# A second block by maxima in one of four graphs, and six generators under way, in the first stage of a four-layer graph network

## The chip, the cores and the metric

The kernel runs on one core of a Trainium2 chip. The metric is the device time in microseconds, the median of several runs. A core has five engines that matter here: TensorE (PE in the profile; its weight loads are shown apart as PEld), VectorE (DVE), ScalarE (ACT), GpSimd (POOL) and SyncE (SP), which only issues transfers. Each engine takes its own instructions strictly in order and waits on semaphores for the others.

## The reference, cut to what matters

Four layers over 128 graphs of 128 nodes with 128 features; each normalizes its input, cuts it at zero and adds a graph layer's result. The change touches only the first half of layer 0, which scores every pair of nodes:

```python
h = jnp.maximum(_layernorm(x, axis=-1), 0.0)
D = jnp.abs(x[:, :, None, :] - x[:, None, :, :])      # x is h here
h = jnp.einsum('bijc,oc->bijo', D, W1) + b1            # 64 outputs for each pair
m = jnp.mean(h, axis=(0, 1, 2))
v = jnp.mean((h - m) ** 2, axis=(0, 1, 2))
h = (h - m) / jnp.sqrt(v + EPS) * g1 + be1
```

The mean and variance go over all pairs of all graphs, so nothing after them can begin until every pair of every graph has been made once. What follows (a leaky relu, a product with W2, a masked softmax, and the three further layers) is the same code before and after.

## The kernel before, in words

The distance is symmetric, so only 127/256 of the ordered pairs of a graph are made: node i with the 63 or 64 nodes after it, cyclically. For that each graph's features, transposed so that features lie on partitions, are kept 192 columns wide in a tile `he`, whose last 64 columns repeat the first 64. A graph's pairs are four blocks `q` of 32 rows each; blocks 0 and 1 are 64 pairs wide (2048 columns), blocks 2 and 3 are 63 (2016).

The first stage has two kinds of generator. `nodes(g)` prepares a group of four graphs: load, normalize (DVE, POOL), transpose (PE into the PSUM tile `pt`), relu on ACT into `he` and once more into `pt`, store to DRAM for later. POOL makes the wrapped columns (`wrapped`, L510 to L512), beside PE's product of the group's features with W1 (`pu`, L496), which ACT and DVE then split into three bf16 parts `us` (L499 to L505). `pairs(b)` handles one graph: its four blocks run as `block(b, q, made)`, and their statistics are put together at the end (L523). The pairs go to DRAM (tile `v`, L526), except for those of the last eight graphs, which stay.

A block is made in one of two ways:

- By differences (blocks 1, 2, 3): DVE (L545) or POOL (L548) subtracts into a tile `d`, ACT takes the absolute value in place (L551), and PE multiplies by W1 (L565, four fp32 matmuls).
- By maxima (block 0): |a - b| = 2 max(a, b) - a - b. DVE makes the maximum (L545, the same instruction form as the subtraction), ACT has nothing to do, and PE multiplies it by 2 W1 and adds the correction -W1 a - W1 b in twelve further bf16 matmuls: the three parts `us` of W1 h, against a constant tile `both` that holds -1 at the two nodes of each pair.

Either way PE leaves 128x1008 or 128x1024 in the PSUM tile `ph`, ACT copies it to `v` (L575), and DVE takes batch statistics of it in two instructions (L580). In every graph DVE makes block 0; in three of four graphs it makes block 2 as well, in the fourth POOL does; POOL makes blocks 1 and 3.

The order of each engine's instructions is fixed while the program is built, by the planner `in_order` (L51): each generator yields an engine, an estimated work time, and the buffers that the step takes and frees; at most `A_UNDER_WAY` generators are open at once; the step that can begin first by these estimates goes next, and the older generator at equal times. Buffers: five `d`, three `ph`, eight `v`, two each of `he`, `pt`, `us`. At run time the order stays as written, with semaphore waits where data or buffers need them.

Of the kernel before, what the change touches and what calls it, by code (L numbers as in the profile page):

```python
# [9 lines left out]
F32 = mybir.dt.float32  # L10
I32 = mybir.dt.int32
I16 = mybir.dt.int16
BF16 = mybir.dt.bfloat16
AF = mybir.ActivationFunctionType
ALU = mybir.AluOpType
# [3 lines left out]
P = 128  # L19
EPS = 1e-5  # L20
NEG = -9000000000000000.0
W = 192
QR = 32
NQ = P // QR
GS = 8
GB = 4
# [6 lines left out]
C_T, C_W, C_V, C_O, C_M = 28, 11, 3, 6, 7  # L33
C_KEPT = {"ps": 1, "t": 6, "w": 3, "v": 1}
A_D = 5
A_UNDER_WAY = 4
A_KEPT = {}
KEEP = 8
B_V, B_R = 8, 3
# [7 lines left out]
PE, ACT, DVE, POOL, DMA = "PE", "ACT", "DVE", "POOL", "DMA"  # L47
# [105 lines left out]
def bcast(ap, pos, n):  # L153

    dims = [list(d) for d in ap.ap]
    return bass.AP(tensor=ap.tensor, offset=ap.offset, ap=dims[:pos] + [[0, n]] + dims[pos:])
# [3 lines left out]
def kernel(ctx: ExitStack, tc: tile.TileContext, x, adj, w, out):  # L160
    nc = tc.nc
# [7 lines left out]
    def cst(name, shape, dtype=F32):  # L169
        return const.tile(shape, dtype, tag=name, name=name)  # L170
# [41 lines left out]
    w1T = cst("w1T", [P, 64])  # L212
# [24 lines left out]
    with tc.tile_pool(name="wload", bufs=2) as wl, tc.tile_pool(  # L237
        name="wps", bufs=2, space=PSUM
# [191 lines left out]
    with tc.tile_pool(name="h_pool", bufs=1) as h_pool, tc.tile_pool(name="pairs", bufs=B_V) as b_v:  # L430
# [10 lines left out]
        with tc.tile_pool(name="a2", bufs=2) as a2, tc.tile_pool(  # L441
            name="a_d", bufs=A_D
        ) as a_d, tc.tile_pool(name="a_ph", bufs=3, space=PSUM) as a_ph, tc.tile_pool(
            name="a_ps", bufs=2, space=PSUM
# [14 lines left out]
            w1T2 = a2.tile([P, 64], F32, tag="w1T2", name="w1T2", bufs=1)  # L459
            nc.vector.tensor_scalar(w1T2, w1T, 2.0, None, ALU.mult)  # L460

            def nodes(g):

                b0 = g * GB
                yield DMA, 0.6, "xg", ""
                xg = a2.tile([P, GB, P], F32, tag="xg", name="xg")
                nc.sync.dma_start(xg, x_t[:, b0 : b0 + GB, :])
                yield DVE, 1.3, "", ""
                s6 = a2.tile([P, GB, 6], F32, tag="ln_s6", name="ln_s6")
                mv = a2.tile([P, GB, 2], F32, tag="ln_mv", name="ln_mv")  # L470
                for i in range(GB):
                    nc.vector.bn_stats(s6[:, i, :], xg[:, i, :])
                    nc.vector.bn_aggr(mv[:, i, :], s6[:, i, :])

                yield POOL, 3.3, "xn", "xg"
                rs = a2.tile([P, GB], F32, tag="ln_rs", name="ln_rs")
                nc.gpsimd.tensor_tensor(rs, mv[:, :, 1], eps, ALU.add)
                nc.gpsimd.tensor_tensor(rs, rs, nhalf, ALU.pow)
                xn = a2.tile([P, GB, P], F32, tag="ln_xn", name="ln_xn")
                nc.gpsimd.tensor_tensor(xn, xg, bcast(mv[:, :, 0], 2, P), ALU.subtract)  # L480
                nc.gpsimd.tensor_tensor(xn, xn, bcast(rs, 2, P), ALU.mult)
                yield PE, 0.45, "pt", "xn"
                pt = a_ps.tile([P, GB, P], F32, tag="pt", name="pt")
                for i in range(GB):
                    nc.tensor.transpose(pt[:, i, :], xn[:, i, :], ident)
                yield ACT, 1.0, "he", ""
                he = a2.tile([P, GB, W], F32, tag="he", name="he")
                nc.scalar.activation(he[:, :, 0:P], pt, AF.Relu)
                nc.sync.dma_start(h_d[g], he[:, :, 0:P])
                nc.scalar.activation(pt, pt, AF.Relu)  # L490
                yield "fork", wrapped(g, he)

                yield PE, 0.9, "ph us", ""
                pu = a_ph.tile([P, GB, 64], F32, tag="ph", name="pu")
                for i in range(GB):
                    nc.tensor.matmul(pu[:, i, :], he[:, i, 0:P], w1T, start=True, stop=True)  # L496
                us = a2.tile([P, 3, GB, 64], BF16, tag="us", name="us")
                yield ACT, 0.31, "", ""
                nc.scalar.copy(us[:, 0], pu)  # L499
                yield DVE, 0.36, "", ""  # L500
                nc.vector.tensor_tensor(pu, pu, us[:, 0], ALU.subtract)
                yield ACT, 0.31, "", ""
                nc.scalar.copy(us[:, 1], pu)
                yield DVE, 0.34, "", "ph"
                nc.vector.tensor_tensor(us[:, 2], pu, us[:, 1], ALU.subtract)  # L505
                yield "join",
                ready[g] = he, pt, us
                yield "done", ("nodes", g)

            def wrapped(g, he):  # L510
                yield POOL, 0.42, "", ""
                nc.gpsimd.tensor_copy(he[:, :, P:W], he[:, :, 0 : W - P])  # L512

            def pairs(b):
                made = {"six": a2.tile([P, 2 * NQ, 6], F32, tag="six", name="six", bufs=4)}
                for q in range(NQ):
                    yield "fork", block(b, q, made)
                yield "join",
                left[b // GB] -= 1
                if not left[b // GB]:  # L520
                    yield "free", "he pt us"
                yield DVE, 0.37, "", ""
                nc.vector.bn_aggr(st[:, b, :], made["six"].rearrange("p a b -> p (a b)"))  # L523
                if b < NB - KEEP:
                    yield DMA, 5.0, "", "v"
                    nc.sync.dma_start(pairs_d[b], made["v"])  # L526
                else:
                    here[b] = made["v"]

            def block(b, q, made):  # L530

                w_, i0, n = width[q], QR * q, 8 * width[q]
                by_dve = q == 0 or (q == 2 and b % 4 != 3)
                yield "after", ("nodes", b // GB)
                yield (DVE, 2.17, "d", "") if by_dve else (POOL, 3.58, "d", "")
                hb, hp, us = (t[..., b % GB, :] for t in ready[b // GB])
                d = a_d.tile([P, QR * 64], F32, tag="d", name="d")  # L540
                dv = d[:, 0 : 4 * n].rearrange("p (i j) -> p i j", j=w_)
                later = shifted(hb[:, i0 + 1 : i0 + 1 + w_], QR)
                if by_dve:
                    own = bcast(hp[:, i0 : i0 + QR], 2, w_)
                    nc.vector.tensor_tensor(dv, later, own, ALU.subtract if q else ALU.max)  # L545
                else:
                    own = bcast(hb[:, i0 : i0 + QR], 2, w_)
                    nc.gpsimd.tensor_tensor(dv, later, own, ALU.subtract)  # L548
                if q:
                    yield ACT, 1.82, "", ""  # L550
                    nc.scalar.activation(d[:, 0 : 4 * n], d[:, 0 : 4 * n], AF.Abs)  # L551
                yield PE, 1.73 if q else 3.15, "ph", "d"
                ph = a_ph.tile([P, 2, 512], F32, tag="ph", name="ph")
                every4 = "p (r x j) -> p x r j"
                by_part = d[:, 0 : 4 * n].rearrange(every4, x=4, j=w_)
                both_by_part = both.rearrange(every4, x=4, j=64)
                for part in range(1 if q else 4):
                    for t in range(2):
                        for a in range(2):
                            k = 2 * t + a  # L560
                            if part == 0:
                                wt, x_ = w1T if q else w1T2, by_part[:, k]
                            else:
                                wt, x_ = us[:, part - 1, :], both_by_part[:, k]
                            nc.tensor.matmul(  # L565
                                ph[64 * a : 64 * a + 64, t, 0:n], wt, x_,
                                start=part == 0, stop=q > 0 or part == 3,
                            )
                if q:
                    yield "after", ("v", b)  # L570
                yield ACT, 0.93, "" if q else "v", "ph"
                if q == 0:
                    made["v"] = b_v.tile([P, NPAIR], F32, tag="v", name="v")
                v = made["v"][:, first[q] : first[q] + 2 * n]
                nc.scalar.copy(v.rearrange("p (t e) -> p t e", t=2), ph[:, :, 0:n])  # L575
                if q == 0:
                    yield "done", ("v", b)
                yield DVE, 1.19, "", ""
                for t in range(2):
                    nc.vector.bn_stats(made["six"][:, 2 * q + t, :], v[:, t * n : t * n + n])  # L580

            ready, left = {}, [GB] * (NB // GB)
# [6 lines left out]
            with tc.manual_schedule(engines=ORDERED):  # L589
                in_order(makers, A_UNDER_WAY, {"d": A_D, "ph": 3, "v": B_V} | two, A_KEPT)  # L590

# [13 lines left out]
            own = a2.tile([P, 1], F32, tag="own", name="own")  # L605
# [4 lines left out]
                start=True, stop=True,  # L610
# [12 lines left out]
        with tc.tile_pool(name="b2", bufs=2) as b2p, tc.tile_pool(name="b_s", bufs=2, space=PSUM) as b_s, tc.tile_pool(  # L623
            name="b_ps", bufs=6, space=PSUM
# [17 lines left out]
                start=True, stop=True,  # L642
# [745 lines left out]
```

## Time and profile before

| what | value |
|---|---|
| median of three runs | 3178.52 us (3177.65 to 3181.38) |
| profiled execution, its own time | 3173.2 us |
| its span, first to last instruction | 3171.4 us |
| first stage: first block's max starts, last graph's statistics end | 40.1 us, 1261.5 us |
| busy in the stage from 40 to 1240 us: PE, DVE, ACT, POOL | 1118.41, 1177.10, 1183.27, 1117.67 of 1200 us |
| instructions in the whole kernel: subtract or max on DVE, on POOL, absolute values | 224, 288, 384 |

Busy time is the union of an engine's instructions: where two overlap, the stretch counts once. The mean of a group is the time of one instruction from start to end, and with pipelining it is longer than the pitch from start to start. "Idle before" is the time in which the engine stood still ahead of an instruction, put down to what came last. In groups, `out<-in` names the tiles, followed by partitions x elements, then the count, busy time and mean.

### The profile page before, as it was taken

Reading aid. Unit: us, or ns where it says so; the run is one execution under the profiler, and the core shown is the slowest. Engines: PE = TensorE matmul, PEld = TensorE weight load, DVE = VectorE, ACT = ScalarE, POOL = GpSimd, SP = SyncE. Lnnn points to the kernel's source line nnn. Section 1 sums busy time; section 2 is a strip of 40 time slices with the busy share of each in tenths; the row PEclk is TensorE's granted clock in tenths of the full one; section 3 lists DMA queues with packets and bytes.
Section 4 is the critical chain, followed back from the end, with each engine's and each line's share of the span. In section 5 each row is a group of like instructions: output and inputs, shape, how many; then the busy total and the mean of one; then the engine's idle time right before and its main releaser. Section 6 shows DMA issues by size and latency. Waiting matters only on the chain.

```text
span 3171.4 us, 46611 instructions
## 1 busy us (share of the span) xinstructions
PE 2832.2 (89%) x17129; PEld 1559.5 (49%) x17129; DVE 2657.7 (84%) x4730; ACT 2673.4 (84%) x3082; POOL 1495.2 (47%) x953
## 2 busy tenths in 40 slices
PE   6999999999999998888888898789999999999996
PEld 2333333333333333233333333367777777877774
DVE  6999999999999998777787787667788878888864
ACT  5999999999999999987787887557877878887774
POOL 5999999999999996111111111122213222212211
PEclk8999999999999999999999998889999999999997
DMA  3555555555555550999999999420111111111000
GB/s 115 226 244 242 240 227 225 243 230 231 240 228 224 237 239 36 373 404 395 401 394 400 404 406 398 151 70 21 51 31 47 42 39 36 54 31 41 11 11 12
DMA packets 150718, 606.46 MB, mean 191 GB/s; under 512 B 15633, under 2 KB 99026, under 8 KB 119762
## 3 DMA queue, kind: packets, MB, share of 16 engines
q1 hardware_dynamic: 140242, 569.86, 45.6%
q0 software_dynamic: 10240, 33.53, 2.9%
q8 instruction: 139, 2.28, 0.3%
q14 instruction: 97, 0.79, 0.1%
HBM read 322.74 MB, written 280.61 MB: 190 GB/s over the span
## 4 chain that ended last, share of the span: by engine, by line
PE 27%; DVE 13%; issue 7%; ACT 5%; POOL 2%; DMA 1%; POOLq 0%; DVEq 0%; ACTq 0%
PE pa L1091 5%; PE sc L698 4%; PE po L1006 2%; DVE p L962 2%; PE z L958 1%; PE ps L1110 1%; PE pl L787 1%; PE pp L1103 1%; PE ph L1233 1%; DMA s<-us 1%; PE pl L789 1%; DVE s L928 1%; DVE v L425 1%; DVE xh L1015 1%; DVE f1d L1194 1%
## 5 line engine op out<-in xcount | busy, mean ns | idle before, releaser
L548 POOL TENSOR_TENSOR d<-he 128x2016 f32<-128x2016 f32 (+1 forms) x288 | 1022.0, 3578 | 77.6 <-ACT v L575 61.7
L565 PE MATMUL ph<-d,w1T 128*64 128x512 f32 (+1 forms) x4096 | 939.8, 596 | 83.1 <-ACT d L551 40.6
L551 ACT ACTIVATE d<-d 128x2016 f32<-128x2016 f32 (+1 forms) x384 | 741.1, 1932 | 0.1
L580 DVE BATCH_NORM_STATS2 six<-v 128x6 f32<-128x504 f32 (+1 forms) x1024 | 631.5, 670 | 8.7 <-ACT v L575 5.1
L565 PEld LDWEIGHTS ph<-d,w1T 128*64 128x64 f32 x4096 | 306.4, 136 | 613.7 <-issue 385.3
L575 ACT COPY v<-ph 128x1024 f32<-128x1024 f32 (+1 forms) x512 | 517.1, 1035 | 14.6 <-PE ph L565 14.6
L545 DVE TENSOR_TENSOR d<-he,pt 128x2048 f32<-128x2048 f32 (+1 forms) x224 | 506.1, 2259 | 13.0 <-PE ph L565 13.0
L935 POOL TENSOR_TENSOR rs<-ve,nhalf 128x4 f32<-128x4 f32 x96 | 120.0, 1250 | 772.2 <-DVE ve L932 558.1
L425 DVE SCALAR_TENSOR_TENSOR v<-v 128x1528 f32<-128x1528 f32 x256 | 433.9, 1742 | 32.8 <-ACT v L653 32.2
L653 ACT ACTIVATE v<-v,h_bi,h_sc 128x1528 f32<-128x1528 f32 x256 | 413.2, 1662 | 6.8 <-DVE h_bi L417 6.8
L698 PE MATMUL sc<-v,w_slide 128*32 128x512 f32 (+1 forms) x1536 | 321.4, 599 | 17.2 <-DVE v L425 16.9
L1091 PE MATMUL pa<-vals,p 128*128 128x99 f32 (+2 forms) x2048 | 254.9, 280 | 14.3 <-DVE p L962 11.1
L1091 PEld LDWEIGHTS pa<-vals,p 128*128 128x128 f32 x2048 | 249.2, 197 | 32.7 <-DVE p L962 15.1
L698 PE MATMUL sc<-v,w_line 128*32 128x504 f32 x512 | 260.3, 590 | 0.0
L698 PE MATMUL sc<-r,w_relu 128*32 128x504 f32 x512 | 258.2, 586 | 0.0
L962 DVE SCALAR_TENSOR_TENSOR p<-p,q 128x1024 f32<-128x1024 f32 (+1 forms) x192 | 206.2, 1081 | 49.5 <-ACT q L1078 24.9
L565 PE MATMUL ph<-both,us 128*64 128x512 bf16 x1536 | 190.5, 381 | 0.0
L1077 ACT ACTIVATE p<-z 128x1024 f32<-128x1024 f32 x128 | 133.2, 1040 | 35.0 <-PE z L958 34.5
L565 PEld LDWEIGHTS <-us 128*64 128x64 bf16 x1536 | 100.9, 111 | 117.7 <-issue 74.6
L660 ACT ACTIVATE r<-v,h_bi,h_sc 128x1008 f32<-128x1008 f32 x128 | 157.4, 1229 | 0.0
L799 ACT ACTIVATE e<-e 128x512 f32<-128x512 f32 x32 | 20.2, 630 | 149.3 <-DVE e L797 149.3
L698 PEld LDWEIGHTS sc<-v,w_slide 128*32 128x32 f32 x1536 | 65.1, 109 | 158.9 <-DVE v L425 82.5
(253 smaller groups left out, 4501.9 us busy)
## 6 DMA issues: line engine op xcount, KB each, us to landing
v<-v SPq DMA_DIRECT2D x240, 2032.0 KB, 9.1
xg<-in_x SPq DMA_DIRECT2D x64, 256.0 KB, 3.1
ht<-h SPq DMA_DIRECT2D x64, 256.0 KB, 6.4
u<-s POOLq DMA_DIRECT2D x16, 768.0 KB, 11.6
h<-he SPq DMA_DIRECT2D x32, 256.0 KB, 3.5
adj<-in_adj SPq DMA_DIRECT2D x32, 256.0 KB, 3.0
adj<-in_adj POOLq DMA_DIRECT2D x32, 256.0 KB, 8.6
y<-yt POOLq DMA_DIRECT2D x32, 256.0 KB, 7.1
```

The costliest lines, as they stand in the source:

```text
L425: engine.scalar_tensor_tensor(out, v, slope, v, ALU.mult, ALU.max)
L545: nc.vector.tensor_tensor(dv, later, own, ALU.subtract if q else ALU.max)
L548: nc.gpsimd.tensor_tensor(dv, later, own, ALU.subtract)
L551: nc.scalar.activation(d[:, 0 : 4 * n], d[:, 0 : 4 * n], AF.Abs)
L565: nc.tensor.matmul(ph[64 * a : 64 * a + 64, t, 0:n], wt, x_, start=part == 0, stop=q > 0 or part == 3,)
L575: nc.scalar.copy(v.rearrange("p (t e) -> p t e", t=2), ph[:, :, 0:n])
L580: nc.vector.bn_stats(made["six"][:, 2 * q + t, :], v[:, t * n : t * n + n])
L653: nc.scalar.activation(part, part, AF.Identity, bias=h_bi, scale=h_sc)
L660: nc.scalar.activation(made["r"][:, 0:n], part, AF.Relu, bias=h_bi, scale=h_sc)
L698: nc.tensor.matmul(sc[rows, 0:n], wz[:, 31 - k : 63 - k], z, start=begins and q < NQ, stop=ends and q != NQ - 1, tile_position=(0, rows.st ...
L962: nc.vector.scalar_tensor_tensor(p, p, FLOOR, q, ALU.max, ALU.max)
L1091: nc.tensor.matmul(pa_all[:, h * (DH + 1) : h * (DH + 1) + n], p[:, h, :], vals_all[:, e : e + n], start=True, stop=True,)
```

## The change

In each group of four graphs, block 1 of the first graph is now also made by maxima. Its correction needs W1 times the graph's nodes turned by 32, so that the same constant tile `both` serves; `pu` and `us` get a fifth part for it, from columns 32 to 159 of `he`, and the wrapped columns must therefore be there first: POOL's copy moves from a branch of its own into the sequence ahead of the `pu` matmuls. The subtractions are shared out anew: DVE makes block 2 in the second and fourth graph of a group, POOL in the first and third. At most six generators are open instead of four, and the statistics tiles `six` have six buffers.

```diff
-A_UNDER_WAY = 4
+A_UNDER_WAY = 6
...
-                yield "fork", wrapped(g, he)
-
-                yield PE, 0.9, "ph us", ""
-                pu = a_ph.tile([P, GB, 64], F32, tag="ph", name="pu")
+                yield POOL, 0.42, "", ""
+                nc.gpsimd.tensor_copy(he[:, :, P:W], he[:, :, 0 : W - P])
+
+
+                yield PE, 1.1, "ph us", ""
+                pu = a_ph.tile([P, GB + 1, 64], F32, tag="ph", name="pu")
                 for i in range(GB):
                     nc.tensor.matmul(pu[:, i, :], he[:, i, 0:P], w1T, start=True, stop=True)
-                us = a2.tile([P, 3, GB, 64], BF16, tag="us", name="us")
+                nc.tensor.matmul(pu[:, GB, :], he[:, 0, QR : QR + P], w1T, start=True, stop=True)
+                us = a2.tile([P, 3, GB + 1, 64], BF16, tag="us", name="us")
...
-                made = {"six": a2.tile([P, 2 * NQ, 6], F32, tag="six", name="six", bufs=4)}
+                made = {"six": a2.tile([P, 2 * NQ, 6], F32, tag="six", name="six", bufs=6)}
...
-                by_dve = q == 0 or (q == 2 and b % 4 != 3)
+                larger = q == 0 or (q == 1 and b % GB == 0)
+                by_dve = larger or (q == 2 and b % 4 in (1, 3))
...
-                hb, hp, us = (t[..., b % GB, :] for t in ready[b // GB])
+                he, pt, us = ready[b // GB]
+                hb, hp, us = he[:, b % GB, :], pt[:, b % GB, :], us[:, :, b % GB if q == 0 else GB, :]
...
-                    nc.vector.tensor_tensor(dv, later, own, ALU.subtract if q else ALU.max)
+                    nc.vector.tensor_tensor(dv, later, own, ALU.max if larger else ALU.subtract)
...
-                if q:
+                if not larger:
                     yield ACT, 1.82, "", ""
                     nc.scalar.activation(d[:, 0 : 4 * n], d[:, 0 : 4 * n], AF.Abs)
-                yield PE, 1.73 if q else 3.15, "ph", "d"
+                yield PE, 3.15 if larger else 1.73, "ph", "d"
...
-                for part in range(1 if q else 4):
+                for part in range(4 if larger else 1):
...
-                                wt, x_ = w1T if q else w1T2, by_part[:, k]
+                                wt, x_ = w1T2 if larger else w1T, by_part[:, k]
...
-                                start=part == 0, stop=q > 0 or part == 3,
+                                start=part == 0, stop=not larger or part == 3,
```

More of the change, by code (lines that the diff above doesn't have):

```diff
@@ L505, in nodes @@
                 nc.vector.tensor_tensor(us[:, 2], pu, us[:, 1], ALU.subtract)
-                yield "join",
                 ready[g] = he, pt, us
                 yield "done", ("nodes", g)
-            def wrapped(g, he):
-                yield POOL, 0.42, "", ""
-                nc.gpsimd.tensor_copy(he[:, :, P:W], he[:, :, 0 : W - P])
             def pairs(b):
-                made = {"six": a2.tile([P, 2 * NQ, 6], F32, tag="six", name="six", bufs=4)}
+                made = {"six": a2.tile([P, 2 * NQ, 6], F32, tag="six", name="six", bufs=6)}
                 for q in range(NQ):
```

## The prediction, made before the result was known

> **What bounds the kernel now.** I read the page's engine line first, then the busy time in stretches, to find the stage that the change touches and what is full there.
>
> ```profile
> PE 2832.2 (89%) x17129; PEld 1559.5 (49%) x17129; DVE 2657.7 (84%) x4730; ACT 2673.4 (84%) x3082; POOL 1495.2 (47%) x953
> ...
> DVE  6999999999999998777787787667788878888864
> ACT  5999999999999999987787887557877878887774
> ```
>
> The diff touches only the first stage, which runs from the first block at 40 us to the last statistics at 1261.5 us. The shares of the whole span mislead: in this stage DVE and ACT are both at 9. The stage is strictly periodic: DVE's only listed wait comes back every 38.00 us (562.67, 600.67, 638.67, ...), once per four graphs. So I take one period, 600.67 to 638.67; the columns are PE, PE weight loads, DVE, ACT, POOL, with instruction counts, then granted clock, DMA share and GB/s:
>
> ```profile
> 600.67:638.67 38.00, 35.49 (x190) 14.13 (x188) 37.47 (x53) 37.62 (x33) 35.44 (x15) 1.00 0.57 234
> ```
>
> ACT is busy 37.62 of 38.00 us and DVE 37.47; PE and POOL have 2.5 us each to spare. The groups of the same period, with forms kept apart (some counts are one too high, an instruction straddling the edge):
>
> ```profile
> L551 ACT ACTIVATE d<-d 128x2016 f32<-128x2016 f32 x8 | 15.3, 1915 | 0.0
> ...
> L545 DVE TENSOR_TENSOR d<-he,pt 128x2048 f32<-128x2048 f32 x4 | 9.1, 2277 | 0.3 <-PE ph L565 0.3
> ...
> L551 ACT ACTIVATE d<-d 128x2048 f32<-128x2048 f32 x4 | 7.8, 1950 | 0.0
> L545 DVE TENSOR_TENSOR d<-he,pt 128x2016 f32<-128x2016 f32 x3 | 6.7, 2238 | 0.0
> ...
> L496 PE MATMUL pu<-w1T,he 128*128 128x64 f32 x8 | 1.1, 281 | 0.0
> ```
>
> The reader sees the two full engines' work and that hardly any of it is preceded by a wait. The waits of the period:
>
> ```profile
> PE ph L565 <- DVE d L545: 1.2, 2, 0.8
> PE ph L565 <- ACT d L551: 1.2, 1, 1.2
> ...
> ACT v L575 <- PE ph L565: 0.4, 1, 0.4
> ...
> DVE d L545 <- PE ph L565: 0.3, 1, 0.3
> ```
>
> DVE's 0.53 us of idle is 0.26 us at one max that waits for PE to release a d buffer, and 0.27 us of small gaps between dependent instructions. PE's 2.5 us are nearly all waits for DVE's and ACT's products.
>
> **What the Trainium skill says.** "VectorE: DVE Perf Modes", section "The TRN2 errata", gives an fp32 two-tensor operation (N+151)/0.96 ns: 2291 ns at 2048 columns; the trace has 2277. Max and subtract are the same instruction form, so exchanging one for the other costs DVE nothing: 2277 and 2238 ns differ by their 2048 and 2016 columns. "TensorE: Matmul & The Clock Gate", "What's actually happening", has the clock halved until PE has been busy for some microseconds, and again after an idle window of about 3.4 us. The trace agrees: 0.50 from 30 to 40 us, then 1.00 for the whole stage, whose longest PE wait is 1.5 us. More PE work will not lower it. "Perfetto Trace Analysis", "Identifying the Most-Contended Engine", trusts occupancy for Vector and Scalar but not for matmuls; so I price PE by the pitch from start to start.
>
> **The change part by part, per period of four graphs.**
>
> *ACT.* One absolute value of 128x2048 goes (block 1 of the first graph): -1.95 us. The two copies of pu become 64 columns wider; at 1.06 ns a column (1038 against 1021 ns for 1024 and 1008) that is +0.14. ACT: 37.62 - 1.95 + 0.14 = 35.81.
>
> *DVE.* The first graph gains a max in block 1 and loses its subtract in block 2 to POOL; the third loses block 2 to POOL; the fourth gains block 2. So 4 maxima + 3 subtracts become 5 + 2: one 2048 for one 2016, +0.04. The two operations on pu are 64 columns wider: the trace's slope is (2277 - 417)/(2048 - 256) = 1.04 ns, so +0.13. Statistics are unchanged. DVE: 37.47 + 0.04 + 0.13 = 37.64.
>
> *POOL.* Nine blocks before (4 of block 1, 1 of block 2, 4 of block 3), nine after (3, 2, 4): one 3603 ns becomes 3558. 35.40.
>
> *PE.* Twelve bf16 correction matmuls are added. In the timeline a maximum block takes 606.14 - 603.11 = 3.03 us from start to start and its fp32 part 1.74, so +1.29 (their busy time alone, 1.48, is the upper end). The fifth pu product is 2 of 8 + 2 instructions: 1.10/8 x 2 = +0.28. PE: 35.49 + 1.57 = 37.06.
>
> So the fullest engine's need goes from 37.62 (ACT) to 37.64 (DVE). ACT's relief does not shorten the bound; it hands it to DVE. What can still be won is DVE's idle 0.53.
>
> *Six generators.* The planner may interleave more graphs; the buffers (5 d, 3 ph, 8 v) stay. In the built order DVE's regular alternation (about two blocks of statistics after each d) gives way to runs of up to four blocks without a d between, and the pattern repeats only after several groups. Such runs mean that copies stand ready and DVE is what is waited for in the plan. Statistics tiles go from 4 to 6 buffers so that this is no wait. Up to five graphs then hold a v tile, and with one or two stores under way (9.1 us to landing, about one graph's 9.5 us) 7 of 8 are used: no cost; were it short, ACT would wait up to 9 us at block 0's copy.
>
> *The moved copy.* POOL's wrap-around copy now stands ahead of the pu matmuls, because the fifth product reads wrapped columns: a new wait of PE on POOL, behind which stand the next blocks' matmuls, and behind them ACT's copies and DVE's free buffers. In the built order PE has one ordinary and one maximum block between the transposes and pu, 1.74 + 3.03 = 4.77 us, where it had one maximum block. In that time ACT needs 0.6 for he, POOL at worst finishes a block (3.58) and copies (0.40): 4.58. Covered by a hair; uncovered it is at most 3.6 us per period, of which PE's slack takes 0.9. SP's loads and stores keep their number, and its DMA share of 0.57 leaves room; I price their new positions at nothing.
>
> *The sum.* I let DVE's listed wait go, since six graphs offer other statistics to fill it, and keep the small gaps, which are latencies of dependent operations: 37.64 + 0.27 = 37.91, or -0.09 per period, -2.9 us over 32 groups. The ends of the stage (5.1 us of DVE waits from 40 to 100 us, 5.6 us after 1100 us) I leave, +-2. Later stages have identical code. Against the profiled execution: 3173.2 us (span 3171.4 and 1.8 around it) becomes 3170.3. The median shown is 5.3 us above that execution, 3178.5, so 3175.6.
>
> **The rivals.** Within 0.2% (6.4 us) is about what a measurement of this kernel cannot tell from no change.
>
> *Filled DVE.* The small gaps were partly waits too, and six generators fill them and the drain: between 37.64 and 37.77 per period, -7 to -11 us, 3169. For it: runs of ready statistics. Against: 0.27 us in some 50 instructions is 5 ns each, hardly a wait.
>
> *PE becomes the second full engine, and the kernel is slower.* PE rises to 37.06 and still waits for DVE's maxima and ACT's absolute values in its fixed order. If its 2.51 us of waits stayed whole, the period would be 39.57, +50 us. It decides from 38.20 on, where PE's waits are still 1.14 us; at 1.5 us the period is 38.56, +18 us, 3196. For it: a maximum block now sometimes follows another closely, and DVE's one listed wait is already for PE. Against: PE's waits came from full ACT and DVE, and ACT now has 2 us to spare.
>
> *ACT's relief does nothing and the waits stay as they are:* 37.64 + 0.53 = 38.17, +5.4 us, 3184; within the bound. That maxima replace absolute values is not in doubt: the built order has 160 of them where there were 128.
>
> **How the numbers follow.** Same bound, DVE in ACT's place (with the rival of unchanged waits): 0.47; its own range 3172 to 3185. Filled DVE: 0.28. PE coupling: 0.25. The likeliest gives 3175.6. The range for 8 in 10 cuts the far end of both others: 3167 to 3194. Faster 0.29, same 0.46, slower 0.25.
>
> **What would show it.** Right: the abs group at 352 and about 62 us less ACT; DVE over 99% in the stage, ACT near 94-95%, PE 97%; bf16 matmuls 1920; a mean of 37.9 us per four graphs; the stage's end within 5 us of 1261.5. Wrong: DVE's waits for PE or ACT's copies at over 0.5 us per four graphs, PE waiting for POOL at pu, or the granted clock under 1.00 inside the stage. A change after 1262 us would mean that I missed a link to the later stages.

## The result, and the profile after

The changed kernel takes 3163.53 us (median of five runs, 3162.32 to 3175.77) where the kernel before took 3181.38 (five runs of the same comparison, 3177.65 to 3186.18): the ratio of the comparison is 0.9958, 95% interval 0.9944 to 0.9973 (the two medians alone, 17.9 us apart, would give 0.9944). It is faster, by 0.42%, some 13 us.

The profiled execution of the changed kernel alone hides this: its span is 3170.4 us, 1.0 less than before. Its first stage ends 13.1 us earlier (the last graph's statistics begin at 1248.06 instead of 1261.14), but the second and third stage, whose code is identical, took 5.8 and 6.2 us longer in this execution (776.6 and 1145.7 us against 770.8 and 1139.5; the border is the third stage's first load on SP). In the 14 profiles of this study these two stages lie between 768 and 781, and between 1136 and 1149 us, without any order by kernel (in one of them the second stage has one load more). So what follows reads the first stage, and in it the time for four graphs in the steady part: the start of the 113th graph's `st` aggregate less that of the 41st, over 18. It is 38.00 us before and 37.71 after.

The changed kernel's page, engine line and the two rows of slices that were shown of before:

```profile
PE 2876.5 (91%) x17577; PEld 1601.7 (51%) x17577; DVE 2655.7 (84%) x4730; ACT 2627.2 (83%) x3050; POOL 1494.6 (47%) x953
...
DVE  6999999999999999768777686577878878888864
ACT  4999999999999998878788787467878778877774
```

ACT lost 46 us and PE gained 44; DVE, the engine that the prediction made the bound, has 2 us less. Now the 18 periods of the steady part, first of the kernel before, then of the changed one (length; busy time of PE, PE's weight loads, DVE, ACT, POOL; granted clock, DMA share, GB/s):

```profile
443.36:1127.36 684.00, 638.85 (x3388) 254.54 (x3384) 674.47 (x956) 677.24 (x577) 638.04 (x253) 1.00 0.57 234
```

```profile
435.68:1114.50 678.82, 657.88 (x3640) 269.91 (x3638) 672.64 (x955) 651.68 (x559) 637.86 (x253) 1.00 0.57 236
```

Divided by 18: PE 35.49 to 36.55, DVE 37.47 to 37.37, ACT 37.62 to 36.20, POOL 35.45 to 35.44. DVE's idle went from 0.53 to 0.34. The groups of the changed kernel in that stretch that answer to those shown of before:

```profile
L552 ACT ACTIVATE d<-d 128x2016 f32<-128x2016 f32 x145 | 276.9, 1914 | 3.1 <-POOL d L549 3.1
...
L546 DVE TENSOR_TENSOR d<-he,pt 128x2048 f32<-128x2048 f32 x90 | 203.9, 2265 | 2.0 <-PE ph L566 2.0
...
L552 ACT ACTIVATE d<-d 128x2048 f32<-128x2048 f32 x54 | 104.2, 1930 | 2.8 <-POOL d L549 2.8
L546 DVE TENSOR_TENSOR d<-he,pt 128x2016 f32<-128x2016 f32 x36 | 80.2, 2228 | 0.0
...
L498 PE MATMUL pu<-w1T,he 128*128 128x64 f32 x144 | 19.9, 281 | 0.0
```

and its waits there (total, times, longest):

```profile
ACT v L576 <- PE ph L566: 17.5, 29, 1.1
...
PE ph L566 <- DVE d L546: 11.7, 18, 1.0
...
PE ph L566 <- DVE us L508: 6.1, 6, 1.0
...
PE ph L566 <- ACT d L552: 3.1, 6, 0.5
...
DVE d L546 <- PE ph L566: 2.0, 6, 0.3
DVE six L581 <- ACT v L576: 1.7, 6, 0.3
```

PE's waits fell from 2.33 us for four graphs (21.1 + 20.8 over 18) to 1.16, and one kind is new: PE waiting for `us` ahead of a correction. ACT waits more, 1.4 us. The pattern now repeats every twelve graphs, 113.1 us, instead of every four.

The rest of the stage's gain lies at its two ends. From the first maximum (40.11 us before, 44.73 after) to the 41st graph the kernel before took 403.25 us with DVE busy 392.93, the changed one 390.95 with 388.08: DVE's idle there fell from 10.3 to 2.9 us. The other 4.9 us is mostly DVE work that the changed order does later: after the 113th graph DVE is busy 131.7 us instead of 127.9 in about the same length, and its idle falls from 6.2 to 2.2. The granted clock is not the reason: it was 0.50 until about 48 us in the profile of before and 1.00 in that of the changed kernel, but a kernel with the written order of before and a clock of 1.00 (less ScalarE, block 1, below) still took 403.21 us from the first maximum to its 41st graph.

The later start gave 4.6 us back. Of this, 2.6 lies before the first normalization, which began at 30.98 instead of 28.42 us, and is not the change's: the same kernel with the order of before began it at 31.00. So the ends in the table below, single executions, carry some 2.6 us of such difference; the period does not.

### The profile page after: what moved, and what is told of

It is laid out like the page before. It is cut to its first block, busy times and chain, and to the rows that moved or that the text cites. A ratio compares the mean times of both kernels' runs of the same rounds, so it can differ in the third digit from the quotient of the medians.

```text
span 3170.4 us, 47435 instructions
## 1 busy us (share of the span) xinstructions
PE 2876.5 (91%) x17577; PEld 1601.7 (51%) x17577; DVE 2655.7 (84%) x4730; ACT 2627.2 (83%) x3050; POOL 1494.6 (47%) x953
## 5 line engine op out<-in xcount | busy, mean ns | idle before, releaser
L566 PE MATMUL ph<-d,w1T 128*64 128x512 f32 (+1 forms) x4096 | 927.2, 595 | 34.6 <-DVE d L546 16.9
L552 ACT ACTIVATE d<-d 128x2016 f32<-128x2016 f32 (+1 forms) x352 | 676.7, 1926 | 13.3 <-POOL d L549 13.2
L581 DVE BATCH_NORM_STATS2 six<-v 128x6 f32<-128x512 f32 (+1 forms) x1024 | 624.0, 669 | 4.4 <-ACT v L576 4.3
L566 PE MATMUL ph<-both,us 128*64 128x512 bf16 x1920 | 236.6, 379 | 0.0
L566 PEld LDWEIGHTS <-us 128*64 128x64 bf16 x1920 | 124.4, 110 | 147.6 <-issue 91.8
L788 PE MATMUL pl<-u,ident 128*128 128x512 f32 x64 | 49.8, 870 | 106.6 <-POOL u L781 106.6
```

The costliest lines, as they stand in the source:

```text
L566: nc.tensor.matmul(ph[64 * a : 64 * a + 64, t, 0:n], wt, x_, start=part == 0, stop=not larger or part == 3,)
```

## The experiments

All periods and ends below come from the profiles of these runs; the times are single ones unless an interval stands beside them. The period is the number to read: it repeats to within 0.01 us in the four kernels whose edit had no effect, while single times of the kernel before lay between 3174.19 and 3191.85 us (23 executions).

| kernel | four graphs, us | last statistics begin, us | time, us |
|---|---|---|---|
| before | 38.00 | 1261.14 | ratio 1 |
| changed | 37.71 | 1248.06 | 0.9958 (0.9944 to 0.9973) |
| changed, four generators | 37.88 | 1257.96 | 0.9973 (0.996 to 0.9987) |
| before, six generators | 37.86 | 1258.56 | 0.9992 (0.998 to 1.0005) |
| changed, less TensorE | 37.43 | 1238.60 | 3156.06 |
| changed, more TensorE | 38.91 | 1282.40 | 3200.11 |
| changed, less VectorE | 37.71 | 1244.16 | 3162.82 |
| changed, less ScalarE | 37.72 | 1245.32 | 3159.97 |
| before, less ScalarE, block 1 | 38.01 | 1263.73 | 3172.32 |
| before, less VectorE, graph 0 | 38.00 | 1263.29 | 3181.64 |
| before, less ScalarE, block 3 | 37.68 | 1254.22 | 3169.33 |
| before, less VectorE, graph 1 | 37.58 | 1249.37 | 3165.93 |
| before, a sixth d buffer | 37.74 | 1253.34 | 3176.74 |
| changed, two correction parts | 37.76 | 1244.90 | 0.9932 (0.9906 to 0.9958) |

### Which half of the change made the gain?

```diff
-A_UNDER_WAY = 6
+A_UNDER_WAY = 4
```

> The changed kernel with four generators under way instead of six (everything else of the change stays). Measured so far: 38.00 us for four graphs in the steady part before, 37.71 after. If the maxima alone make the gain (relief of ScalarE), 37.7 again and a time within 3 us of the changed kernel. If the deeper interleaving is needed to fill VectorE, the period goes back to 37.9 to 38.3 and the time to within 5 us of the kernel before, or above it.

And the other half alone, in the kernel before:

```diff
-A_UNDER_WAY = 4
+A_UNDER_WAY = 6
...
-                made = {"six": a2.tile([P, 2 * NQ, 6], F32, tag="six", name="six", bufs=4)}
+                made = {"six": a2.tile([P, 2 * NQ, 6], F32, tag="six", name="six", bufs=6)}
```

> The kernel before with six generators and six statistics buffers, nothing else. ScalarE still needs 37.62 us for four graphs. If the interleaving alone makes the gain, the period is 37.7 and the time about 13 us under before. If ScalarE's relief is needed as well, the period stays at 37.9 to 38.1 and the time within 5 us of before.

Measured: 37.88 and 37.86 us. Neither theory holds: each half brings a part, 0.12 and 0.14 us, and both together 0.29. In whole times the maxima alone gave 0.27% and the six generators alone nothing that can be told from no change. The stretch from the first maximum to the 41st graph splits in the same way: 398.4 us with the maxima alone and 397.7 with six generators alone, against 403.25 before and 390.95 with both. What holds the kernel in that stretch was not traced.

### Is TensorE a second full engine after the change?

The written order stays as in the changed kernel; the twelve corrections of the new maximum block are left out, or issued twice.

```diff
-for part in range(4 if larger else 1):
+for part in range(4 if q == 0 else 1):
...
-start=part == 0, stop=not larger or part == 3,
+start=part == 0, stop=q > 0 or part == 3,
```

> The changed kernel in the same written order, with the twelve bf16 correction matmuls of the second maximum block left out (that block's values are wrong). TensorE loses 1.29 us for four graphs. If VectorE bounds the stage, the period stays at 37.71 within 0.05, the stage's end within 2 us. If TensorE had become a second full engine, the period falls by 0.2 us or more, the stage's end by 6 us or more.

```diff
-for part in range(4 if larger else 1):
+parts = [0, 1, 2, 3] + [1, 2, 3] * (q == 1) if larger else [0]
+for m, part in enumerate(parts):
...
-start=part == 0, stop=not larger or part == 3,
+start=m == 0, stop=m == len(parts) - 1,
```

> The changed kernel in the same written order, with those twelve correction matmuls issued twice (that block's values are wrong). TensorE needs about 36.5 + 1.3 = 37.8 us for four graphs. If TensorE has no room left the period rises by the whole 1.29 us (41 us in all). If it has the 1 us that the trace of the changed kernel shows idle, the period rises by 0.3 to 0.6 us (10 to 20 us in all).

The steady part of the two (less, then more TensorE):

```profile
432.37:1106.03 673.66, 638.13 (x3424) 254.10 (x3422) 671.16 (x956) 648.02 (x560) 637.49 (x253) 1.00 0.58 237
```

```profile
445.08:1145.47 700.39, 681.15 (x3854) 285.55 (x3852) 674.76 (x955) 654.33 (x559) 638.98 (x253) 1.00 0.56 228
```

Twelve more matmuls cost 1.20 of their 1.29 us, near the theory without room: PE has next to none at this place, although the trace shows it idle for 1.16 us in each period. Its waits hardly shrink under the load: for DVE's maxima, `us` and ACT's absolute values they were 11.7, 6.1 and 3.1 us, and with the doubled corrections

```profile
PE ph L567 <- DVE d L546: 10.0, 18, 0.7
PE ph L567 <- DVE us L508: 6.1, 6, 1.0
PE ph L567 <- ACT d L552: 3.1, 6, 0.5
```

Twelve fewer give only 0.29, and then DVE is busy 671.16 of 673.66 us with no listed wait left but small gaps of 2.5 us in the normalization. So 37.43 is what DVE needs in this order, and the changed kernel stands 0.29 above it: the second corrections are part of what holds it there. Whether PE's work at another place would count as much was not tried.

### Do VectorE and ScalarE hold the changed kernel?

```diff
-v[:, t * n : t * n + n]
+v[:, t * n : t * n + (8 if t and q == 3 and b % 4 == 0 else n)]
```

> The changed kernel in the same written order; the second statistics instruction of block 3 in the first graph of each group reads 8 columns instead of 504 (its statistics are wrong), 0.52 us less of VectorE for four graphs. If VectorE still sets the pace, the period falls from 37.71 by 0.4 to 0.5. If TensorE alone does, by less than 0.1. If the two are coupled through TensorE's waits for VectorE's maxima, something between.

```diff
+na = 8 if q == 1 and b % 4 == 1 else 4 * n
-nc.scalar.activation(d[:, 0 : 4 * n], d[:, 0 : 4 * n], AF.Abs)
+nc.scalar.activation(d[:, 0:na], d[:, 0:na], AF.Abs)
```

> The changed kernel in the same written order; one more absolute value for four graphs (block 1 of the second graph) covers 8 columns only (its values are wrong), 1.7 to 1.9 us less of ScalarE. If ScalarE has stopped being a bound, the period stays at 37.71 within 0.1. If its copies still decide, it falls by 0.2 or more.

DVE's busy time fell by 0.45 us a period (664.56 over 18 against 672.64) and ACT's by 1.52 (624.32 against 651.68). The period moved by 0.00 in both. For ACT that was expected if it was no bound any more. For DVE it is the number of the theory in which TensorE's chain alone sets the pace, but it does not prove that theory (the trace of the changed kernel, followed below, contradicts it). It does show that an engine that is busy 99% of the time does not by that set the pace.

### Did they hold the kernel before?

The same two edits in the kernel before, the absolute value in block 1 of the first graph:

```diff
+na = 8 if q == 1 and b % 4 == 0 else 4 * n
```

> The kernel before in its own written order; the absolute value of block 1 in the first graph of each group covers 8 columns only (its values are wrong): the relief of ScalarE alone, without more TensorE work. If ScalarE alone held the kernel before at 38.00, the period falls to VectorE's need, 37.5 to 37.65. If the two are equally full, to 37.7 to 37.9.

> The kernel before in its own written order; the same narrowed statistics instruction as in the other run, 0.52 us less of VectorE for four graphs (its statistics are wrong). If ScalarE holds the kernel before (37.62 busy), the period falls by no more than 0.15, to 37.85 or above. If VectorE holds it too, by 0.2 to 0.4.

Again nothing: 38.01 and 38.00, although ACT lost 1.59 us a period and DVE 0.52. PE's two waits of before stand in the kernel with less ScalarE too, to the tenth:

```profile
PE ph L566 <- DVE d L545: 21.1, 36, 0.8
PE ph L566 <- ACT d L552: 20.8, 18, 1.2
```

With less ScalarE neither theory's number came (37.5 to 37.65, or 37.7 to 37.9). With less VectorE the 38.00 is what the theory of a full ScalarE said, but the other run refutes that theory. Two full engines that each take over where the other is relieved would fit both numbers as well; the two runs of the next section rule that out. So the premise falls that the fullest engines bound the stage. The timeline of the kernel before shows what does. Followed from wait to wait, first on DVE, then PE, then ACT (start, length, what; in brackets the idle time ahead):

```profile
600.67 2.29 DVE L545 TENSOR_TENSOR d<-he,pt 128x2048 f32<-128x2048 f32 x1 [0.26 <-PE ph L565]
...
609.40 2.27 DVE L545 TENSOR_TENSOR d<-he,pt 128x2048 f32<-128x2048 f32 x1
```

```profile
603.11 1.94 PE L565 MATMUL ph<-d,w1T 128*64 128x512 f32 x8 [0.84 <-DVE d L545]
...
611.82 1.94 PE L565 MATMUL ph<-d,w1T 128*64 128x512 f32 x8 [0.33 <-DVE d L545]
...
614.85 3.63 PE L565 MATMUL ph<-d,w1T 128*64 128x504 f32 x16
619.63 1.93 PE L565 MATMUL ph<-d,w1T 128*64 128x504 f32 x8 [1.16 <-ACT d L551]
```

```profile
616.80 1.00 ACT L575 COPY v<-ph 128x1008 f32<-128x1008 f32 x1 [0.38 <-PE ph L565]
617.69 1.89 ACT L551 ACTIVATE d<-d 128x2016 f32<-128x2016 f32 x1
```

It is one closed chain. DVE's maximum at 600.67 waits until PE has finished a block and so released a `d` buffer. DVE then works without a gap to the end of the next maximum, 611.67 (11.0 us). PE starts on it at 611.82 and finishes the block after it at about 616.75, where ACT's wait for it ends (4.9 us). ACT copies that, takes the next absolute value until 619.58 (2.8 us), and PE starts on that at 619.63 and works without a gap; at about 638.6 (19.0 us) it ends the block that frees the buffer for the maximum at 638.67, and the chain begins anew. 11.0 + 4.9 + 2.8 + 19.0 and four handovers of some 0.1 us are the 38.00 us. PE has 24 of them, ACT only 2.8. Neither of the two narrowed instructions lies on it: in this period ACT's would stand at about 613.5 us and DVE's at about 625.6.

### The same work, but on the chain

```diff
-na = 8 if q == 1 and b % 4 == 0 else 4 * n
+na = 8 if q == 3 and b % 4 == 0 else 4 * n
```

> The kernel before, same written order; the absolute value of block 3 in the first graph of each group covers 8 columns only (its values are wrong). It is the one that TensorE waits for (1.16 us) in the trace of before, and the same work as the one narrowed without effect in block 1. If the period of before is set by one closed chain through three engines, it falls from 38.00 by 0.3 to 1.0. If ScalarE's work does not matter anywhere, it stays at 38.00.

```diff
-v[:, t * n : t * n + (8 if t and q == 3 and b % 4 == 0 else n)]
+v[:, t * n : t * n + (8 if t and q == 3 and b % 4 == 1 else n)]
```

> The kernel before, same written order; the second statistics instruction of block 3 in the second graph of each group reads 8 columns (its statistics are wrong): the same 0.52 us of VectorE as in the run without effect, but between the two maxima that TensorE waits for. If the closed chain sets the period, it falls by 0.2 to 0.5. If VectorE's work does not matter anywhere, it stays at 38.00.

37.68 and 37.58: -0.32 and -0.42, where the same kind of work elsewhere gave 0.00. In the second ACT is then busy 676.19 of 676.44 us: only here does the fullest engine itself set the pace. In the first PE's wait for an absolute value is gone, and only this is left:

```profile
PE ph L566 <- DVE d L545: 39.9, 54, 1.4
```

### The chain's link through the buffers

```diff
-KEEP = 8
-B_V, B_R = 8, 3
+KEEP = 7
+B_V, B_R = 7, 3
...
-            name="a_d", bufs=A_D
+            name="a_d", bufs=A_D + 1
```

> The kernel before, in the same written order of its first stage, with six d buffers at run time where the planner counts five; for the room, seven v tiles and seven graphs kept instead of eight (one more pair tile is stored and loaded again). If the closed chain passes through the release of d buffers by TensorE, the period falls from 38.00 to 37.6 to 37.8 and VectorE's wait for TensorE at a maximum is gone. If buffers do not matter, it stays at 38.00.

37.74 us, -0.26: one more buffer opens the link. (The edit also takes away a `v` tile; fewer tiles can add waits, but not shorten the period.) PE's wait for an absolute value stays, its wait for maxima falls from 21.1 to 13.3 us, and DVE's wait for PE at a maximum is no longer listed:

```profile
PE ph L565 <- ACT d L551: 20.8, 18, 1.2
...
PE ph L565 <- DVE d L545: 13.3, 36, 0.5
```

That fits the Trainium skill, "Perfetto Trace Analysis", section "Optimization Strategy": a gap that comes back at the same place, on an engine that should be full, can mean too few buffers. Here the gap was 0.26 us, once in every 38.00.

The trace of the changed kernel, followed in the same way, closes too, after twelve graphs:

```profile
662.63 2.29 DVE L546 TENSOR_TENSOR d<-he,pt 128x2048 f32<-128x2048 f32 x1 [0.33 <-PE ph L566]
682.45 1.94 PE L566 MATMUL ph<-d,w1T 128*64 128x512 f32 x8 [0.69 <-DVE d L546]
700.87 14.15 POOL L549 TENSOR_TENSOR d<-he 128x2016 f32<-128x2016 f32 x4 [2.53 <-PE ph L566]
729.01 1.91 ACT L552 ACTIVATE d<-d 128x2048 f32<-128x2048 f32 x1 [0.46 <-POOL d L549]
736.45 1.29 DVE L581 BATCH_NORM_STATS2 six<-v 128x6 f32<-128x512 f32 x2 [0.28 <-ACT v L576]
759.10 1.94 PE L566 MATMUL ph<-d,w1T 128*64 128x512 f32 x8 [0.30 <-DVE d L546]
775.77 2.29 DVE L546 TENSOR_TENSOR d<-he,pt 128x2048 f32<-128x2048 f32 x1 [0.33 <-PE ph L566]
```

Between one line and the next the engine works without a wait: DVE 19.7 us, PE 18.4 (it then frees a `d` buffer for POOL), POOL 28.1, ACT 7.4, DVE 22.5, PE 16.6 (it frees a `d` buffer for DVE). With six handovers these are the 113.1 us; DVE has 42 of them and PE 35, so it is not TensorE's chain alone. The statistics instruction narrowed without effect lies on neither of the two DVE stretches, which have the same lengths in that run. The absolute value narrowed without effect is the one at 729.01, on the chain. With it narrowed, DVE's wait for ACT's copy is gone, but the maximum that follows waits 0.21 us for PE instead: another chain of nearly the same length takes over, so 1.5 us less of ScalarE gave nothing.

### Less TensorE and VectorE work in a changed order

With TensorE taken to hold the changed kernel, the third bf16 part of the corrections was dropped in all maximum blocks, with the DVE operation that makes it.

```diff
-us = a2.tile([P, 3, GB + 1, 64], BF16, tag="us", name="us")
+us = a2.tile([P, 2, GB + 1, 64], BF16, tag="us", name="us")
...
-yield ACT, 0.31, "", ""
+yield ACT, 0.31, "", "ph"
...
-yield DVE, 0.34, "", "ph"
-nc.vector.tensor_tensor(us[:, 2], pu, us[:, 1], ALU.subtract)
...
-yield PE, 3.15 if larger else 1.73, "ph", "d"
+yield PE, 2.68 if larger else 1.73, "ph", "d"
...
-for part in range(4 if larger else 1):
+for part in range(3 if larger else 1):
...
-start=part == 0, stop=not larger or part == 3,
+start=part == 0, stop=not larger or part == 2,
```

> The changed kernel with the corrections in two bf16 parts instead of three (the third part, below 2^-16 of the value, is left out): 4 of 12 correction matmuls less in each of five maximum blocks for four graphs, about 2.1 us of TensorE, and one VectorE operation of 0.48 us less for each group; the planner's estimate for such a block is lowered to match. If TensorE's chain and VectorE set the pace together, the period falls to VectorE's remaining need: 37.43 (the run without the second block's corrections) less 0.45, about 37.0, some 22 us of the whole. If other waits hold, it stays above 37.4.

The period is 37.76, not 37.0: PE did 1.84 us less in it (624.69 against 657.88 over 18) and waited that much more, for ACT's copies to release `ph`:

```profile
PE ph L564 <- ACT v L574: 31.2, 19, 2.8
PE ph L564 <- POOL d L547: 10.6, 9, 1.2
PE ph L564 <- DVE d L544: 10.5, 18, 1.0
```

The steady part of the changed kernel lists no such wait of its matmuls. The new order, written for other estimates, has its own chain, it seems through the three `ph` tiles. The whole time, 3162.55 us median of four (ratio 0.9932, 0.9906 to 0.9958), can't be told from the changed kernel's. Whether the same cut in the changed kernel's order would reach 37.0 was not tried.

## Why the prediction was right or wrong

The forecast was 3175.6 us, 2.9 under the median then known; measured were 13 us. Laid on the same 3178.5, the ratio gives 3165.2 (3160.7 to 3169.9), just below the range 3167 to 3194, which its interval overlaps. The likeliest case (within 0.2%, 0.47) did not come. The period of the rival "Filled DVE" (0.28: 37.64 to 37.77 us, -7 to -11 us in all) did, with 37.71, but by luck: DVE was not filled to a need of 37.64, it was busy 37.37 and still stood idle for 0.34. That the forecast had the right sign is luck too, for the sum behind it does not describe what set either period.

- **"So the fullest engine's need goes from 37.62 (ACT) to 37.64 (DVE)."** This is the step that failed. The need of the fullest engine was not what set the 38.00: taking 1.59 us from ACT or 0.52 from DVE in the kernel before changed nothing, and the same kind of cut at another place, or a sixth buffer, did. The steady part was held by a closed chain through DVE, PE, ACT and the `d` buffers, and after the change by chains that close only after twelve graphs. The idle of an engine at 99% was read as all that can be won, which is right as a limit, but not as the place where to look.
- **DVE 37.64.** Measured 37.37. The additions were right (the two operations on `pu` 488 and 475 ns against 417 and 420, +0.13), but the same work took 0.27 less than the sum. DVE's busy time is not a fixed sum: with the same instructions in the same order it was 37.29, 37.37 and 37.49 us a period as PE's load was cut, left and raised. No run isolated why.
- **Gaps 0.27 and the listed wait.** I let the wait of 0.26 go and kept the gaps of 0.27. Instead 0.21 of waits (2.0 + 1.7 over 18) and 0.13 of gaps remained: the gaps in the normalization stayed, those ahead of the statistics went. "Hardly a wait", said of the gaps, was half wrong.
- **ACT 35.81.** Measured 36.20. An absolute value was priced at its mean, 1.95 us, but instructions overlap, and taking it out saved only some 1.5 of busy time (1.42, and 0.06 more that the wider copies added: 7.7 + 7.6 over 18 against 0.79). Without effect on the period, as the runs with less ScalarE show.
- **PE 37.06.** Measured 36.55. The corrections' 1.29 held where they were doubled (681.15 - 657.88 over 18), but leaving them out took only 1.10 away (657.88 - 638.13 over 18); the rest of PE's work took 0.3 to 0.5 us less busy time than the sum has it.
- **POOL 35.40.** Measured 35.44.
- **The moved copy, "covered by a hair".** Covered: PE lists no wait for POOL at `pu`. But `us`, one step further, now ends late enough that PE waits for it (6.1 us in 18 periods). I had not followed the chain that far. The same wait appears with six generators alone (8.9 us), so the copy is not its only cause.
- **"PE becomes the second full engine, and the kernel is slower."** Half of it is so: PE's waits did stay, and more work at the second corrections lengthens the period. The rival put the border of slower at 38.20, where PE's waits are 1.14 us. They are 1.16, and the kernel is still faster, because PE's busy part came out 0.5 us smaller than priced.
- **The ends of the stage, "+-2".** This is the term that made the size wrong. DVE's idle up to the 41st graph fell by 7.4 us and that after the 113th by 4.0; the 18 steady periods gave 5.2 in all. The forecast priced these ends at nothing, although it had 5.1 and 5.6 us of waits there in hand.
- **The clock, "1.00 for the whole stage".** Before the change it was still 0.50 in the stage's first 8 us. As shown above, this made no difference.
- **"What would show it".** The shares forecast for being right came, or nearly (in the steady part DVE 99%, PE 97%, and ACT 96% where 94 to 95% were forecast), none of the listed signs of being wrong did, and yet the period and the stage's end were missed. Shares of busy time could not tell a DVE bound from a closed chain.
- **Later stages identical.** The code is; one execution of them differs by some 6 us from another, which is why one profiled span could not confirm the gain.

## What to carry to other kernels

When several engines are nearly full (here four, at 93 to 99%), the pace can be set by a closed chain that hands work round and returns through a released buffer; an engine's share of busy time then says little about what relieving it is worth. Follow the repeating waits until they close, and price an edit by whether its instructions lie on that chain: the same 0.5 us of VectorE was worth 0.42 on it and 0.00 beside it. When an edit on the chain gives nothing, look for a second chain of the same length. Before crediting a change to one of its parts, run the parts alone: here each gave under half.

## What the runs showed of the hardware that was not expected

- TensorE's visible idle was no room at the place tried: at 36.55 busy of 37.71 us, 1.29 us of further matmuls lengthened the period by 1.20.
- VectorE's busy time for the same instructions in the same order differed by 0.2 us in 37.4 as TensorE's load was cut, left or raised.
- ScalarE at 37.62 of 38.00 us could lose 1.59 us at one place without any effect, and 0.32 us of the period went with the same kind of cut at another. The Trainium skill, "Perfetto Trace Analysis", section "Identifying the Most-Contended Engine", would have the engine with the highest occupancy optimized first; in this stage that alone was not enough, since the place decided.
